# A fused attention and gated projection layer on one core: half steps filled by kind, and shift rows that go through DRAM

## The chip, the core and the metric

The kernel runs on one core of a Trainium2 chip, as one program. It uses the core's five engines: TensorE (PE) for matmuls, ScalarE (ACT) for activations, VectorE (DVE), GpSimd (POOL), and SyncE (SP), which here issues every DMA. The metric is the device time of one execution in microseconds; for the kernel before it is the median of three runs, 5673.93 us (5659.39 to 5677.47).

## What is computed

The input x has 8 batches of 2048 tokens with 512 channels in float32. The layer is, cut to what matters:

```
xn   = layernorm(x)                                  # over the 512 channels
q, k = xn Wq + bq, xn Wk + bk                        # 8 heads, 8 channels each
v    = xn Wv + bv                                    # 8 heads, 64 channels each
s    = leaky(q k^T / sqrt(8), slope 0.2)             # 2048 x 2048 per head
att  = gamma * softmax(s) v + xn
gate = softmax over 4 experts of a normalized projection of xn; only the largest is kept
g    = silu(xn W + sum over experts of gate * (xn Wd Wu))
out  = x + att * g
```

## The kernel before

**Tiling.** A block is 512 tokens, four to a batch (`NB`). Heads are taken in pairs, four to a batch (`NPAIR`). A *sequence* is one batch, one block of queries and one pair of heads: 16 a batch, 128 in all. A sequence runs over 16 *chunks* of 128 keys (`CH`). The main loop therefore has 2048 steps, one for each sequence s and chunk i.

**One step.** TensorE runs `less_max` for the first head of the pair (L658, adds the negated row maximum to the scores in PSUM), the scores of the next chunk (L641), the two matmuls of `max_unit` (L587, scores for a sequence further on, of which only the row maxima are kept by VectorE, L598), and `less_max` for the second head. ScalarE then takes exp of both heads (L670) and applies the leaky slope to the next scores (L652). The next step's `less_max` waits for that. Until then TensorE has time for other work: this is the *half step*. GpSimd adds each chunk's exponentials into the denominators (L702).

**What fills the half step.** First the *values* of earlier chunks: `weigh` multiplies exp scores by v (L682, one chunk is one matmul for each head) and may lag; chunks not yet weighed stand in the list `last`. Second, work from three queues of generators: `ending(s)` (denominators dps, L725; transposes of the result atp, L742; four VectorE operations, L744 to L749; output), `shift_rows` (below), and the background `behind()`, which runs through two kinds of blocks. `project_block` prepares the next batch: layer norm, transposes tp (L362, VectorE copy L365, ScalarE `normalize` L310), queries and keys (qkps, L257, split by VectorE at L323 and L326 and stored to DRAM), and values (vps, L271). `lift_block` computes g for one block of the current batch: pps (L257), norms nps (L422), dps (L257), gate gps (L443 and small VectorE operations), ranks rps (L490 and three VectorE operations L493, L496, L499), and four times zps (L271 and L510, then tanh th on ScalarE L513 and g on VectorE L514). All of these results pass through the one PSUM buffer of the pool `ps_m`, tag "m".

**Who decides.** A generator yields a state at each place where it may be interrupted: HOLD (in the middle of a chain of matmuls), WAIT (goes on at the next half step), FREE, SLOW, or IDLE (not yet). `background` steps through the queues until an estimated cost of 1.6 us is spent or the planner's due time (`due_at`, from a list of tasks with costs and ends) is met. The main loop then weighs zero, one or two chunks by what `background` spent. When loading of the next stacks (`load_stacks`, at i = 0 for sequence s + 2) finds that batch's keys not yet stored, it calls `background(force=True)` until they are. Layer norm statistics of the next block (`norm`: bn_stats L295 and L296) are advanced behind each vps and zps job through `following`.

**Shift rows.** For each sequence, `shift_rows` turns the row maxima (128 tokens on partitions) into rows along the free axis, split into a high and a low part. VectorE reduces (L604, L610, L611), GpSimd splits (L612 to L617), TensorE transposes the 128x16 result into PSUM (cps, L622), VectorE copies it to SBUF (cT, L624), and eight DMAs from SP lay it into the tile `shift` (L630). `less_max` of that sequence reads the tile.

**Order.** The order of instructions on each engine is the order in which the program issues them. A queue works strictly in order, so an instruction that waits holds everything behind it on its engine. SP likewise issues its DMAs in order.

Of the kernel before, what the change touches and what calls it, by code (L numbers as in the profile page):

```python
# [32 lines left out]
def fused_layer_kernel(  # L33
# [66 lines left out]

    xtiles = {}
# [54 lines left out]
    nc.gpsimd.memset(rx, 0.0)  # L156
    ones_r = const.tile([128, 128], FR, name="ones_r")
# [76 lines left out]

    EARLY = 9
    SLOW, WAIT, HOLD, FREE, IDLE = 4, 3, 2, 1, 0
# [46 lines left out]
    normed = {}  # L283
    ready = []
# [67 lines left out]
    def project_block(b, n, following, prefetch):  # L352

        if (b, n) not in normed:
            for _ in norm(b, n):
                pass
        xn, normalize = normed.pop((b, n))
        xnT = two.tile([128, NC, BLK], FP, name="xnT")
        for t in range(NT):
# [7 lines left out]
            yield FREE  # L367
# [20 lines left out]
        for t in range(NT):  # L388
            ps = bank([128, C], "vps")
            yield from token_major(ps, wv_sb, columns(xnT), t)  # L390
            add_bias(vb, t, ps)
            next(following, None)
            yield FREE
# [3 lines left out]
        if not prefetch:  # L397
            for _ in following:
                yield FREE
            yield FREE  # L400

    def lift_block(b, n, following, prefetch, cols=None):
# [16 lines left out]
        yield FREE  # L419
# [20 lines left out]
        yield FREE  # L440
# [45 lines left out]
        yield FREE  # L486
# [6 lines left out]
        nc.vector.tensor_tensor(rps, rps, dn, ALU.mult)  # L493
        dst = one.tile([128, BLK], FR, name="dst")
# [3 lines left out]
        )  # L498
        nc.vector.tensor_tensor(dst[64:128, :], rps[64:128, :], hi[64:128, :], ALU.subtract)  # L499
        spend(0.5)  # L500
        yield WAIT
        nc.scalar.copy(dst[0:64, :], hi[0:64, :])
        yield WAIT

        g = one.tile([128, NT, C], FP, name="g")
        for t in range(NT):
# [8 lines left out]
            next(following, None)  # L515
            yield SLOW
        nc.sync.dma_start(out=GS[b][n], in_=g)
        lifted.append((b, n))
        if not prefetch:
            for _ in following:  # L520
                yield FREE
            yield FREE
# [10 lines left out]
    def load_stacks(s):  # L533
# [4 lines left out]
        while b > 0 and b not in ready:  # L538
            background(force=True)
# [15 lines left out]
    def load_values(s):  # L555
# [3 lines left out]
        while b not in valued:  # L559
            background(force=True)  # L560
# [39 lines left out]
    def shift_rows(s):  # L600
# [7 lines left out]
        c = sm.tile([128, 2, 2 * NT], FP, name="c")  # L608
# [11 lines left out]
        yield FREE  # L620
        cps = ps_m.tile([4 * NT, 128], FP, name="cps", tag="m")
        nc.tensor.transpose(cps, c.rearrange("p i m -> p (i m)"), ident)  # L622
        cT = sm.tile([4 * NT, 128], FP, name="cT")
        nc.vector.tensor_copy(cT, cps)  # L624
        spend(0.45)
        shift = qp.tile([128, BLK], FR, name="shift")
        for g in range(4):
            for i in range(2):
                o = 2 * NT * i + NT * (g % 2)
                nc.sync.dma_start(  # L630
# [455 lines left out]
```

## Time and profile before

| what | value |
|---|---|
| median of three runs | 5673.93 us |
| profiled execution | 5658.03 us |
| its span, first to last instruction | 5656.3 us |
| TensorE busy | 5390.9 us, 95% |
| GpSimd busy | 4783.9 us, 85% |
| ScalarE busy | 4454.6 us, 79% |
| VectorE busy | 3643.2 us, 64% |
| DMA queue of SP | 35.4% of 16 engines, 109 GB/s |
| granted TensorE clock, mean | 0.978 |

In the profile, a row of instructions names the line of the kernel, the engine, the operation and the tiles (output <- inputs), then how often it ran, its busy time and the mean of one, and the idle time of the engine just before such instructions with what ended it. In the timeline, the first column is the start in microseconds from the span's start, the second the duration of the (merged) instructions; in brackets stands the idle time before and what released it. A float32 matmul shows two records for each instruction, so one chunk of values shows as four rows of L682, and two matmuls of a projection as four. A view by windows gives, for each stretch: its length, busy time of PE, PEld, DVE, ACT and POOL with the number of instructions in brackets, then the granted clock, the DMA share and GB/s.

### The profile page before, as it was taken

The page shows a single profiled execution, that of the slowest core. Times are in us where ns is not written, and L with a number is a line of the kernel's source. Part 1 is how long each engine was busy: PE and PEld are TensorE (multiplying, and loading weights), DVE is VectorE, ACT ScalarE, POOL GpSimd, SP SyncE. Part 2 cuts the span into 40 slices and gives each one's busy share as a digit, 9 for nine tenths or more (in the row PEclk, how much of TensorE's full clock was granted, in tenths as well). Part 3 has the DMA queues.
Part 4 walks back from the last instruction along what each step waited for, and adds up shares of the span by engine and source line. Part 5 has one row for each costly group of instructions (what it writes and reads, how often), then busy time and mean ns, then how long its engine had stood idle before and what let it go on. Part 6 is the DMA issues. An engine that isn't in the chain of part 4 may idle for free.

```text
span 5656.3 us, 78627 instructions
## 1 busy us (share of the span) xinstructions
PE 5390.9 (95%) x26386; PEld 1975.0 (35%) x26386; DVE 3643.2 (64%) x4988; ACT 4454.6 (79%) x8627; POOL 4783.9 (85%) x2904
## 2 busy tenths in 40 slices
PE   8899999999999999999999999999999999999998
PEld 3333333333333333333333333333333333333332
DVE  5566666667666665676666666667666666665664
ACT  2788878888788887888778887888878888777787
POOL 1789888888788987889788888888888898788888
PEclk9899999999999999999999999999999999999998
DMA  5324342343423333333333334233353243422221
GB/s 189 111 77 153 105 136 77 98 144 99 123 88 115 116 114 112 98 101 126 114 107 95 118 114 144 94 87 122 96 148 106 70 149 93 136 79 82 71 76 59
DMA packets 518026, 614.34 MB, mean 109 GB/s; under 512 B 30780, under 2 KB 429116, under 8 KB 481528
## 3 DMA queue, kind: packets, MB, share of 16 engines
q1 hardware_dynamic: 517624, 609.32, 35.4%
q8 instruction: 210, 3.44, 0.3%
q14 instruction: 192, 1.57, 0.1%
HBM read 405.79 MB, written 201.33 MB: 107 GB/s over the span
## 4 chain that ended last, share of the span: by engine, by line
PE 65%; DVE 16%; ACT 9%; issue 6%; POOL 2%; DMA 1%; SPq 0%; DVEq 0%; POOLq 0%; ACTq 0%
PE av L682 20%; PE sc L658 12%; PE vps L271 8%; PE zps L271 8%; PE mx L587 6%; DVE mxr L598 5%; ACT ex L670 5%; ACT sc L652 3%; PE qkps L257 3%; PE dps L257 2%; PE pps L257 2%; DVE gs L749 2%; DVE atp L748 2%; POOL acc L702 1%; DVE atp L744 1%
## 5 line engine op out<-in xcount | busy, mean ns | idle before, releaser
L702 POOL TENSOR_TENSOR acc<-acc,ex 128x1024 f32<-128x1024 f32 x1792 | 4236.9, 2364 | 294.8 <-ACT ex L670 201.8
L598 DVE TENSOR_REDUCE mxr<-mx 128x2 f32<-128x1024 f32 x2032 | 2481.7, 1221 | 1449.8 <-PE sc L658 1019.0
L670 ACT ACTIVATE ex<-sc 128x512 f32<-128x512 f32 x4096 | 2236.3, 597 | 962.3 <-PE sc L658 806.2
L652 ACT ACTIVATE sc<-sc 128x512 f32<-128x512 f32 x4096 | 2235.6, 592 | 20.1 <-PE sc L641 20.1
L682 PE MATMUL av<-ex,v_sb 128*64 128x512 f32 x8192 | 2122.0, 618 | 0.7
L658 PE MATMUL sc<-shift,ones_r 2*128 2x512 f32 x4096 | 1633.4, 458 | 74.3 <-ACT sc L652 70.3
L587 PE MATMUL mx<-k,q_sb 32*128 32x512 f32 x4096 | 1430.4, 449 | 27.7 <-DVE mxr L598 22.6
L658 PEld LDWEIGHTS sc<-shift,ones_r 2*128 2x128 f32 x4096 | 687.8, 185 | 1757.3 <-ACT sc L652 1696.0
L641 PE MATMUL sc<-q_sb,k 32*128 32x512 f32 x4096 | 1029.7, 499 | 0.0
L682 PEld LDWEIGHTS av<-ex,v_sb 128*64 128x64 f32 x8192 | 453.9, 136 | 775.0 <-issue 752.3
L587 PEld LDWEIGHTS mx<-k,q_sb 32*128 32x128 f32 x4096 | 563.7, 185 | 72.2 <-DVE mxr L598 57.1
L271 PE MATMUL zps<-w_sb,xnT 128*128 128x512 f32 (+1 forms) x1120 | 550.1, 606 | 16.9 <-DMA xnT<-XT 10.5
L702 POOL TENSOR_TENSOR acc<-ex 128x1024 f32<-128x1024 f32 x128 | 302.1, 2360 | 266.3 <-ACT ex L670 266.2
L271 PE MATMUL vps<-wv_sb,xnT 128*128 128x512 f32 x960 | 485.7, 627 | 12.2 <-DVE lo L326 10.8
L641 PEld LDWEIGHTS sc<-q_sb,k 32*128 32x128 f32 x4096 | 382.5, 183 | 0.8 <-issue 0.8
L271 PEld LDWEIGHTS zps<-w_sb,xnT 128*128 128x128 f32 x1120 | 190.4, 194 | 259.3 <-issue 192.4
L271 PEld LDWEIGHTS vps<-wv_sb,xnT 128*128 128x128 f32 x960 | 163.3, 190 | 217.2 <-issue 193.4
L514 DVE SCALAR_TENSOR_TENSOR g<-th,zps 128x512 f32<-128x512 f32 x128 | 88.0, 688 | 177.2 <-ACT th L513 177.2
L612 POOL TENSOR_TENSOR ml<-m,big 128x8 f32<-128x8 f32 x128 | 26.2, 205 | 144.3 <-DVE m L611 144.3
L257 PE MATMUL qkps<-xnT,wqk_sb 128*128 128x512 f32 x240 | 138.9, 716 | 7.6 <-DVE xnT L365 5.5
L257 PE MATMUL dps<-xnT,wd_sb 128*128 128x512 f32 (+1 forms) x280 | 135.0, 596 | 0.0
L257 PE MATMUL pps<-xnT,wp_sb 128*128 128x512 f32 (+1 forms) x280 | 133.4, 588 | 0.7
(125 smaller groups left out, 2648.4 us busy)
## 6 DMA issues: line engine op xcount, KB each, us to landing
v_sb<-VS SPq DMA_DIRECT2D x127, 1024.0 KB
k<-KS SPq DMA_DIRECT2D x256, 256.0 KB
XN<-xn SPq DMA_DIRECT2D x32, 1024.0 KB
q_sb<-QS SPq DMA_DIRECT2D x256, 128.0 KB
xnT<-XT SPq DMA_DIRECT2D x32, 1024.0 KB
GS<-g SPq DMA_DIRECT2D x32, 1024.0 KB
gs<-GS SPq DMA_DIRECT2D x128, 256.0 KB
xs<-in_x_dram SPq DMA_DIRECT2D x128, 256.0 KB
```

The costliest lines, as they stand in the source:

```text
L257: nc.tensor.matmul(ps[:, part], lhsT=wt[:, c, :], rhs=xnT[c][:, part], start=(c == 0 and part.start == 0), stop=(c == NC - 1 and part.stop ...
L271: nc.tensor.matmul(ps[:, part], lhsT=xnT[c][:, t * 128 : (t + 1) * 128], rhs=wt[:, c, part], start=(c == 0 and part.start == 0), stop=(c = ...
L587: nc.tensor.matmul(parts[e], lhsT=q_sb[r, t * 128 : (t + 1) * 128], rhs=k_sb[r, kb // 2 * BLK : (kb // 2 + 1) * BLK], start=True, stop=True,)
L598: nc.vector.reduce_max(mxr[s][:, :, t, kb : kb + 1], mx, axis=AX.X)
L641: nc.tensor.matmul(sc[e], lhsT=k_sb[r, i // 2 * 128 : (i // 2 + 1) * 128], rhs=q_sb[r, :], start=True, stop=True,)
L652: nc.scalar.activation(sc[e], sc[e], AF.Prelu, alpha=SLOPE)
L658: nc.tensor.matmul(sc[e], lhsT=ones_r[r, :], rhs=shifts[s][r, :], start=False, stop=True, skip_group_check=True,)
L670: nc.scalar.activation(ex[:, e, :], sc[e], AF.Exp, scale=qscale)
L682: nc.tensor.matmul(avt[s][64 * e : 64 * e + DV, :], lhsT=v_sb[:, i, 64 * e : 64 * e + DV], rhs=ex[:, e, :], start=(i == 0), stop=(i == CH ...
L702: nc.gpsimd.tensor_tensor(acc[s], old, ex, ALU.add)
L748: nc.vector.tensor_tensor(tp, tp, gs, ALU.mult)
L749: nc.vector.tensor_tensor(gs, tp, xs[:, 0], ALU.add)
```

## The change

The rule by which half steps are filled is replaced by two functions. In all but the last batch `half_full` decides by the kind of what is next: a WAIT piece goes on and one or two chunks are weighed; a small piece (new state TINY) comes behind one chunk of values; otherwise the half holds either two matmuls of a chain or two chunks of values. After a finished piece, values come first (`ended`). In the last batch `half_light` weighs about one chunk each step and fills up to 0.8 us of estimated cost. Layer norm statistics are kept in `stats` and advanced only in halves of values. `ranks` in `lift_block` is spread over two WAIT states more evenly: product, high part, low part. `load_stacks(s + 2)` may come at i = 0 to 3, and the queue is forced only at i = 3. The planner's allowance per sequence (`END`) goes from 1.45 to 1.0.

In `shift_rows` the TensorE transpose and the copy out of PSUM go away. VectorE transposes the tile `parts` in blocks of 32x32 (only 16 of its 32 columns are used), four DMAs write the result to a DRAM tile `SH`, and four DMAs read it back as rows.

The diff, cut to its core:

```diff
+    SH = [tc.dram_tile([2, 2, NT, 4, 32], FP, name=f"SH{i}") for i in range(2)]
...
-    SLOW, WAIT, HOLD, FREE, IDLE = 4, 3, 2, 1, 0
+    TINY, SLOW, WAIT, HOLD, FREE, IDLE = 5, 4, 3, 2, 1, 0
...
 (project_block)
-        if (b, n) not in normed:
-            for _ in norm(b, n):
-                pass
+        for _ in stats.pop((b, n)):
+            pass
...
-            yield FREE
+            yield TINY if t + 1 < NT else FREE
...
             add_bias(vb, t, ps)
-            next(following, None)
-            yield FREE
+            yield FREE if prefetch or t + 1 < NT else TINY
...
 (lift_block: before nps, before gps, before rps)
-        yield FREE
+        yield TINY
...
         nc.vector.tensor_tensor(rps, rps, dn, ALU.mult)
+        spend(0.5)
+        yield WAIT
...
+        yield WAIT
         nc.vector.tensor_tensor(dst[64:128, :], rps[64:128, :], hi[64:128, :], ALU.subtract)
-        spend(0.5)
-        yield WAIT
         nc.scalar.copy(dst[0:64, :], hi[0:64, :])
-        yield WAIT
+        yield HOLD
...
             nc.vector.scalar_tensor_tensor(g[:, t, :], th, 1.0, ps, ALU.add, ALU.mult)
-            next(following, None)
-            yield SLOW
+            yield SLOW if prefetch or t + 1 < NT else TINY
...
 (shift_rows)
-        c = sm.tile([128, 2, 2 * NT], FP, name="c")
+        c = parts[s % 2][:, 0 : 4 * NT].rearrange("p (i m) -> p i m", i=2)
...
-        yield FREE
-        cps = ps_m.tile([4 * NT, 128], FP, name="cps", tag="m")
-        nc.tensor.transpose(cps, c.rearrange("p i m -> p (i m)"), ident)
-        cT = sm.tile([4 * NT, 128], FP, name="cT")
-        nc.vector.tensor_copy(cT, cps)
-        spend(0.45)
+        cT = sm.tile([128, 32], FP, name="cT")
+        nc.vector.transpose(cT, parts[s % 2])
+        for q in range(4):
+            nc.sync.dma_start(
+                out=SH[s % 2][:, :, :, q, :].rearrange("i e t j -> (i e t) j"),
+                in_=cT[32 * q : 32 * q + 4 * NT, :],
+            )
         shift = qp.tile([128, BLK], FR, name="shift")
         for g in range(4):
-            for i in range(2):
-                o = 2 * NT * i + NT * (g % 2)
-                nc.sync.dma_start(
-                    out=shift[STK * g + i : STK * g + i + 1, :].bitcast(FP), in_=cT[o : o + NT, :]
-                )
+            nc.sync.dma_start(
+                out=shift[STK * g : STK * g + 2, :].bitcast(FP),
+                in_=SH[s % 2][:, g % 2].rearrange("i t q j -> i (t q j)"),
+            )
...
 (ending: the two states FREE become TINY)
...
+    def ahead():
+        return holder or [k for k in (1, 0, 2) if queue[k] is not None and state[k] != IDLE]
+
+    def go_on():
+        for j in range(3):
+            if queue[j] is not None and state[j] == IDLE:
+                go(j)
+        if holder and state[holder[0]] == WAIT:
+            go(holder[0])
+            return True
+        return False
+
+    def force():
+        j = ahead()[0] if ahead() else 2
+        go(j)
+
+    def values(count):
+        for w in last[:count]:
+            weigh(*w)
+        del last[:count]
+
+    def half_full():
+        run = 0
+        for w in last[:2]:
+            run += 1
+            if w[1] == CH - 1:
+                break
+        alone = run and last[0][1] == CH - 1
+        if go_on():
+            values(run)
+            return
+        j = (ahead() or [None])[0]
+        if j == 2 and state[2] != HOLD and spent[0] > due[0] + AHEAD:
+            j = None
+        if j is not None and state[j] == TINY:
+            values(min(run, 1))
+            go(j)
+            ended[0] = True
+        elif j is None or len(last) > MUCH - (state[j] != HOLD) or (ended[0] and run > 1):
+            ended[0] = False
+            for g in stats.values():
+                next(g, None)
+            values(run)
+        else:
+            if alone:
+                values(1)
+            go(j)
+            if state[j] == HOLD and not alone:
+                go(j)
+            ended[0] = state[j] != HOLD
+
+    def half_light():
+        begun = spent[0]
+        go_on()
+        late = last and (state[2] == SLOW or last[0][1] == CH - 1)
+        if late:
+            values(1)
+        j = (ahead() or [None])[0]
+        while j is not None and state[j] != WAIT and spent[0] < begun + 0.8 and (j < 2 or spent[0] < due[0]):
+            go(j)
+            if state[j] != HOLD:
+                break
+        if not late:
+            values(2 if spent[0] - begun < 0.4 and len(last) > 1 and last[0][1] < CH - 1 else 1)
+
+    MUCH, AHEAD = 3, 6.0
...
-    END = 1.45
+    END = 1.0
...
-                if i == 0:
+                if i <= 3 and s + 2 not in qst and (where(s + 2)[0] in (0, *ready) or i == 3):
                     load_stacks(s + 2)
...
+                if s < (B - 1) * SEQ:
+                    half_full()
                 else:
+                    half_light()
```

## The prediction

> **What bounds the kernel now.** I read the page first: shares by engine, then the groups.
>
> ```profile
> span 5656.3 us, 78627 instructions
> PE 5390.9 (95%) x26386; PEld 1975.0 (35%) x26386; DVE 3643.2 (64%) x4988; ACT 4454.6 (79%) x8627; POOL 4783.9 (85%) x2904
> L702 POOL TENSOR_TENSOR acc<-acc,ex 128x1024 f32<-128x1024 f32 x1792 | 4236.9, 2364 | 294.8 <-ACT ex L670 201.8
> L630 SPq DMA_DIRECT2D shift<-cT x1024: 572/573/1599, 127.8 to 5593.2; - x171
> ```
>
> TensorE looks full and GpSimd nearly so. But busy shares say little here, since matmuls overlap. So I cut the trace into the 2048 steps of the main loop: a step runs from one first `less_max` (L658) to the next, and its length is the distance between their starts. The first starts at 135.5 us, the last at 5639.6, and 16.6 us follow. The timeline shows three kinds. First two matmuls of a projection, then two chunks of values (TensorE alone):
>
> ```profile
> 569.03 0.49 PE L658 MATMUL sc<-shift,ones_r 2*128 2x512 f32 x1
> 569.69 1.99 PE L257 MATMUL pps<-xnT,wp_sb 128*128 128x512 f32 x4
> 571.61 0.49 PE L658 MATMUL sc<-shift,ones_r 2*128 2x512 f32 x1
> 572.27 1.94 PE L682 MATMUL av<-ex,v_sb 128*64 128x512 f32 x8
> 574.14 0.49 PE L658 MATMUL sc<-shift,ones_r 2*128 2x512 f32 x1
> ```
>
> 571.61 - 569.03 = 2.58 us, then 2.53: TensorE sets these. A step with one chunk alone:
>
> ```profile
> 941.30 0.49 PE L658 MATMUL sc<-shift,ones_r 2*128 2x512 f32 x1
> 941.89 1.09 ACT L670 ACTIVATE ex<-sc 128x512 f32<-128x512 f32 x2 [0.19 <-PE sc L658]
> 942.18 1.08 PE L682 MATMUL av<-ex,v_sb 128*64 128x512 f32 x4
> 942.86 1.09 ACT L652 ACTIVATE sc<-sc 128x512 f32<-128x512 f32 x2
> 943.52 0.50 PE L658 MATMUL sc<-shift,ones_r 2*128 2x512 f32 x1 [0.26 <-ACT sc L652]
> ```
>
> It takes 2.22 us, and its end is set by ScalarE (exp, then the leaky step of the next scores). So a step costs about 2.22 us however little TensorE has, and 2.55 with a full half. Last, a half step in which the queue is forced (start of a batch's last load of stacks), TensorE alone:
>
> ```profile
> 738.41 1.94 PE L682 MATMUL av<-ex,v_sb 128*64 128x512 f32 x8
> 740.93 0.66 PE L362 MATMUL tp<-ident,xn 128*128 128x128 f32 x4 [0.58 <-ACT xn L310]
> 742.46 0.63 PE L362 MATMUL tp<-ident,xn 128*128 128x128 f32 x4 [0.87 <-DVE xnT L365]
> ...
> 747.79 6.54 PE L257 MATMUL qkps<-xnT,wqk_sb 128*128 128x512 f32 x8 [0.78 <-DVE xnT L365]
> 754.26 0.50 PE L658 MATMUL sc<-shift,ones_r 2*128 2x512 f32 x1
> ```
>
> 754.26 - 737.51 = 16.75 us for one step; it occurs seven times.
>
> **The method.** I counted, in the order of instructions of both built programs, what each half step holds, and gave each kind the median length it has in this trace. The median is free of stalls; what actual lengths have over it is the stall. For the bulk, steps 16 to 1791 (sequences 1 to 111, up to the last batch):
>
> - two chunks, 2.53 us: 491 before, 613 after
> - two matmuls, 2.585: 431, 489; with L510 behind them, 2.81: 67, 93
> - a chunk and a matmul (some with L510), 2.73 to 2.96: 195, 30
> - a chunk and a small piece: 500, 418
> - a chunk alone, 2.22: 85, 103
> - one matmul (some with L510), 2.3 to 2.4 (estimate: the ScalarE floor and a little): 0, 30
> - forced: 7, 0
>
> **Part 1, the half steps by kind.** After, 613 x 2.53 + 489 x 2.585 + 93 x 2.81 + 30 x 2.73 + 103 x 2.22 + 30 x 2.36 = 3458 us. The 418 small ones: transposes of the input 84 x 2.66 + 28 x 2.36 (ScalarE's L310 is added there), denominators and final transposes 222 x 2.25, norms 28 x 2.7, gate 28 x 2.66, ranks 28 x 2.25 = 1002. Together 4460 us. Two of these kinds stand in the trace only the other way round (final transposes and ranks ahead of the chunk); their shortest cases, 2.24 and 2.26, are the price. The same sum for before is 4470: **the stall-free work is the same**, because the 128 removed L622 transposes lie in steps that ScalarE ends anyway. The actual bulk is 4782, so 312 us are stalls, and what the change is worth is how many go.
>
> - Forced halves: 7 x 16.45 - 7 x 2.53 = 97 us, and 18 in the steps behind them (L271 waits for L326). After, no half holds more than three matmuls: loading of stacks may wait until the fourth step of a sequence, and the program is never forced. Gone: 115.
> - Small piece ahead of the chunk: denominators 2.53 (91 of them), against 2.25 where the chunk is ahead (20): the small matmuls wait for VectorE or for the one PSUM bank "m", with the chunk behind them. All are turned round: 91 x 0.28 = 25 us; final transposes 2.51 against 2.25, 111 x 0.26 = 29; L622, 91 x 0.16 = 15. Gone: some 69.
> - Bank "m" and VectorE after a job's end: pairs of zps matmuls cost 52 us over price, 33 of it behind ranks (three 0.69 us VectorE operations in one go; the maxima's L598 comes late, and L587 waits for it). After, they are spread over three halves, every finished piece is followed by values, and bn_stats stand behind L598 instead of ahead. Of the 128 left (312 - 115 - 69) I take about 30 to remain.
> - New stalls: after denominators come final transposes at once, then four 0.69 us VectorE operations in two steps, in the steps where L604 to L611 also run: 2.96 + 2.8 us of VectorE against 2.25 + 2.53 of step, less about 0.6 of slack: 0.4 us x 111 = 45. Long runs of light steps, below: 25.
>
> Bulk after: 4460 + 30 + 45 + 25 = **4560**, 222 less. The last 255 steps are 666 us now. Priced with the medians of that stretch (half-size matmul and chunk 2.40), after comes to 610, and I leave 25 of stalls: 635, 31 less. Sequence 0 stays at about 55 us: its 15.4 us step waits for the load of xnT, which is untouched.
>
> [...]
>
> ```profile
> 737.00:757.00 20.00, 14.48 (x49) 6.37 (x46) 6.59 (x9) 8.14 (x15) 8.40 (x6) 0.74 0.43 152
> 1000.00:1040.00 40.00, 38.89 (x211) 14.80 (x207) 27.33 (x47) 33.13 (x66) 35.95 (x24) 1.00 0.36 106
> ```
>
> The column behind the brackets is the granted clock: 0.74 in a forced stretch, 1.00 in a normal one. In the trace's clock records it is halved 34 times; in light runs a lone chunk then takes 3.06 us for 2.22 and the first pair of matmuls up to 5.1 for 2.6. [...] If each of the 28 blocks fell, 28 x (3 x 0.84 + 2.5) = 140 us. But 13 runs of six light steps in the bulk now show no fall, and of 22 pairs of idlest steps one does. I take 25 us, five falls.
>
> **Part 2, the shift rows.** Removed per sequence: L622 (0.27 us), L624 (0.27), eight DMAs. Added: a 128x32 block transpose on VectorE (between L604's 0.19 and L624's 0.27; hidden, VectorE is at 64%), four DMAs to DRAM, a wait on SP for them, four back. At 0.62 us from issue to issue and 1.4 from an issue to its landing (L630 in the trace), the path is 4 x 0.62 + 1.4 + 4 x 0.62 + 1.4 = 7.8 us, 6.4 before. In the programs' order it now starts always in the tenth step; before, in the 11th to 14th. Six steps, 15 us, are left until the next sequence's first `less_max`. Queued behind SP's wait are stacks and values needed seven steps or more later. Cost nothing; without that cover, 127 x the lateness. Before the loop nothing covers it: +2 us.
>
> **GpSimd** does not take over: L702 queued starts every 2.44 us; 15 x 2.44 + 1.5 for L612 to L617 + 0.7 for norms = 38.8 us a sequence, against 4560 / 111 = 41.1.
>
> **Sum** against the profiled execution: 5656.3 - 222 - 31 + 2 = 5405 us of span. The execution took 5658.0, the median of the runs is 5673.9; keeping some of that distance, **5415 us**.
>
> **The rivals.**
> 1. The clock falls in most light runs (140 for 25): 5530. [...] Chance 0.15.
> 2. VectorE is late every sequence: denominators with final transposes right behind now cost 3.02 us for 2.25 (19 cases). If that stays, 111 x 0.77 = 85 for 45, and as much again in the maxima: 5455 to 5540, say 5500. The chunk between them (0.86 us) speaks against. Chance 0.08.
> 3. Slower: the round trip of the shift rows ends after the sequence. It has 7 us of slack; behind a burst of block stores (3 MB at 400 GB/s, 8 us, some two sequences a batch) it is used up. The gain of 251 is gone if all 127 sequences are 2 us late, at 17 us from transpose to landing; at 20 us, 5415 + 127 x 5 = 6050. Chance 0.07.
> 4. No change: forced work only moves, with its stalls (spread halves that wait for the same banks): 5670. Chance 0.03.
>
> The rest, 0.67, is the forecast, with 5340 to 5490 as its own range. The range over all but 2 in 10 is 5335 to 5550. About 0.3% is what a measurement can tell: faster 0.90, same 0.03, slower 0.07.
>
> **What would show it.** Right: no step over 6 us behind sequence 0; granted clock 0.99 in the bulk; no wait of L587 for L598 behind ranks; denominators and final transposes at 2.25. Wrong: L657, the new line of `less_max`, waiting for a DMA at each sequence's start; half clock in light runs; steps of pure pairs longer than 2.6.

## The result and the profile after

The changed kernel takes 5629.96 us (median of five runs, 5619.18 to 5640.99) against 5673.93 us: a ratio of 0.9927, 95% interval 0.9906 to 0.9948. It is faster, as forecast, but by 44 us where 259 were forecast, and it lies 80 us above the range.

First the page of the changed kernel: span, busy shares, the granted clock in 40 slices, and the group of the denominators' adds.

```profile
span 5617.4 us, 78032 instructions
PE 5378.9 (96%) x26258; PEld 1999.1 (36%) x26258; DVE 3673.9 (65%) x4988; ACT 4440.7 (79%) x8627; POOL 4779.1 (85%) x2906
PEclk9999999999999999999999999999999999979989
L701 POOL TENSOR_TENSOR acc<-acc,ex 128x1024 f32<-128x1024 f32 x1792 | 4231.0, 2361 | 301.7 <-ACT ex L669 189.3
```

The busy shares have hardly moved. TensorE's busy time fell by 12 us only, although 128 transposes (35 us) are gone: more of its work ran at half clock (mean granted clock 0.968, before 0.978). The same cut into steps as in the prediction (from one first `less_max`, now L657, to the next), in us:

| stretch | before | predicted | after |
|---|---|---|---|
| to the first step | 135.5 | 137.5 | 131.2 |
| sequence 0 | 55.9 | 55 | 59.9 |
| bulk, steps 16 to 1791 | 4781.8 | 4560 | 4702.8 |
| last 255 steps | 666.4 | 635 | 704.8 |
| tail | 16.6 | 17 | 18.8 |
| span | 5656.3 | 5405 | 5617.4 |

So the missing 212 us lie in two places: 143 in the bulk and 70 in the last batch. With the prediction's prices the bulk's steps come to 4461 us, so that 241 us of stalls are left, where 100 were allowed. (That the sum agrees with the 4460 forecast tests little, since counts and prices are the forecast's own. With the medians of the changed kernel's trace the same steps come to 4517: some 57 of the 241 us are steps that are dearer in the median.) The seven forced half steps of 16.45 us are gone. But steps over 6 us are not. In six sequences of the bulk one step takes 7.4 to 8.9 us. Here is one of them in the timeline of the changed kernel (start, duration):

```profile
2062.25 1.48 SPq L717 DMA_DIRECT2D xs<-XN  x1
...
2065.55 0.70 DVE L743 TENSOR_TENSOR atp<-atp,rd 128x512 f32<-128x512 f32 x1
...
2067.99 0.49 PE L657 MATMUL sc<-shift,ones_r 2*128 2x512 f32 x1
...
2069.69 0.70 DVE L744 TENSOR_TENSOR atp<-atp,xs 128x512 f32<-128x512 f32 x1 [3.43 <-DMA xs<-XN]
2070.29 1.22 DVE L597 TENSOR_REDUCE mxr<-mx 128x2 f32<-128x1024 f32 x1
2071.57 0.80 PE L586 MATMUL mx<-k,q_sb 32*128 32x512 f32 x2 [3.08 <-DVE mxr L597]
...
2072.71 3.68 PE L681 MATMUL av<-ex,v_sb 128*64 128x512 f32 x8
...
2076.32 0.79 PE L657 MATMUL sc<-shift,ones_r 2*128 2x512 f32 x1
```

The step is 2076.32 - 2067.99 = 8.33 us. An ending reads `gs` and `xs` back from DRAM (L714 to L717). Between 2053 and 2059 us SP has just issued the stores of a whole block (KS, QS, XN, XT), and this read, issued at 2062.25, is waited for until 2069.69. Behind the 3.43 us of this wait VectorE does L744 and then the row maxima (L597, at 2070.29), which need nothing of the read. TensorE's next maxima (L586) wait 3.08 us for those, and then two chunks take 3.68 us for 1.94, at a granted clock of 0.50. In the view of waits (us in total, times, longest) of the kernel before, where VectorE waits for no such read, and then of the changed kernel:

```profile
PE mx L587 <- DVE mxr L598: 22.6, 69, 0.7
```

```profile
PE mx L586 <- DVE mxr L597: 35.9, 20, 3.7
...
DVE atp L744 <- DMA xs<-XN: 25.9, 8, 4.0
```

In the last batch it is another wait. The timeline of the changed kernel around one gate and ranks:

```profile
5016.13 0.69 DVE L748 TENSOR_TENSOR gs<-atp,xs 128x512 f32<-128x512 f32 x1
...
5016.97 1.84 PE L446 MATMUL gps<-simn,pw 128*128 128x4 f32 x8 [3.02 <-DVE gs L748]
...
5018.74 1.98 PE L681 MATMUL av<-ex,v_sb 128*64 128x512 f32 x4
...
5020.64 0.79 PE L657 MATMUL sc<-shift,ones_r 2*128 2x512 f32 x1
...
5027.38 1.12 PE L493 MATMUL rps<-ident,rx 128*128 128x128 f32 x4 [2.45 <-DVE rx L479]
```

`half_light` lets the ending's last two VectorE operations and the gate's first matmuls fall into one half. Both need the one PSUM bank "m". TensorE waits 3.02 us with the chunk behind the gate, then runs at a granted clock of 0.50: one chunk takes 1.98 us for 1.08. The steps with norms, gate and ranks take 6.0 to 7.6 us each here, 2.3 to 4.2 before.

The shift rows, on the other hand, are in time. Timeline of the changed kernel, one round trip:

```profile
5023.04 0.20 DVE L621 STREAM_TRANSPOSE cT<-c 128x32 f32<-128x32 f32 x1
...
5023.27 1.70 SPq L623 DMA_DIRECT2D SH<-cT  x4
...
5026.09 1.11 SPq L629 DMA_DIRECT2D shift<-SH  x4
```

The last read is issued 4.2 us after the start of the transpose. No `less_max` waits for a DMA anywhere in the view of waits.

### The profile page after: what moved, and what is told of

It is laid out like the page before. It is cut to its first block, busy times and chain, and to the rows that moved or that the text cites. A ratio compares the mean times of both kernels' runs of the same rounds, so it can differ in the third digit from the quotient of the medians.

```text
span 5617.4 us, 78032 instructions
## 1 busy us (share of the span) xinstructions
PE 5378.9 (96%) x26258; PEld 1999.1 (36%) x26258; DVE 3673.9 (65%) x4988; ACT 4440.7 (79%) x8627; POOL 4779.1 (85%) x2906
## 4 chain that ended last, share of the span: by engine, by line
PE 80%; ACT 8%; DVE 7%; DMA 2%; issue 2%; SPq 1%; POOL 1%; POOLq 0%; ACTq 0%; DVEq 0%
PE av L681 28%; PE sc L657 16%; PE zps L279 9%; PE vps L279 8%; PE mx L586 7%; ACT ex L669 5%; ACT sc L651 2%; PE pps L265 2%; DVE mxr L597 2%; PE qkps L265 2%; PE dps L265 2%; PE dps L724 1%; DMA xs<-XN 1%; PE atp L741 1%; DVE gs L748 1%
## 5 line engine op out<-in xcount | busy, mean ns | idle before, releaser
L597 DVE TENSOR_REDUCE mxr<-mx 128x2 f32<-128x1024 f32 x2032 | 2480.2, 1221 | 1260.0 <-PE sc L657 1018.5
L681 PE MATMUL av<-ex,v_sb 128*64 128x512 f32 x8192 | 2149.5, 630 | 11.6 <-DVE avs L708 9.2
L657 PE MATMUL sc<-shift,ones_r 2*128 2x512 f32 x4096 | 1679.7, 463 | 75.5 <-ACT sc L651 66.9
L586 PE MATMUL mx<-k,q_sb 32*128 32x512 f32 x4096 | 1445.4, 454 | 37.0 <-DVE mxr L597 35.9
L657 PEld LDWEIGHTS sc<-shift,ones_r 2*128 2x128 f32 x4096 | 703.6, 187 | 1560.4 <-ACT sc L651 1450.5
L681 PEld LDWEIGHTS av<-ex,v_sb 128*64 128x64 f32 x8192 | 469.7, 138 | 839.6 <-issue 805.2
L586 PEld LDWEIGHTS mx<-k,q_sb 32*128 32x128 f32 x4096 | 562.2, 188 | 61.2 <-DVE mxr L597 49.4
L349 DVE TENSOR_TENSOR vb<-vps,bv_sb 128x512 f32<-128x512 f32 x120 | 83.0, 691 | 95.6 <-PE vps L279 95.4
```

The lines of the kernel that those rows point to most:

```text
L349: nc.vector.tensor_tensor(vb[:, :, t, :], ps.rearrange("p (h d) -> p h d", h=NPAIR), bv_sb.rearrange("p (h d) -> p h d", h=NPAIR), ALU.add,)
L586: nc.tensor.matmul(parts[e], lhsT=q_sb[r, t * 128 : (t + 1) * 128], rhs=k_sb[r, kb // 2 * BLK : (kb // 2 + 1) * BLK], start=True, stop=True,)
L597: nc.vector.reduce_max(mxr[s][:, :, t, kb : kb + 1], mx, axis=AX.X)
L657: nc.tensor.matmul(sc[e], lhsT=ones_r[r, :], rhs=shifts[s][r, :], start=False, stop=True, skip_group_check=True,)
L681: nc.tensor.matmul(avt[s][64 * e : 64 * e + DV, :], lhsT=v_sb[:, i, 64 * e : 64 * e + DV], rhs=ex[:, e, :], start=(i == 0), stop=(i == CH ...
```

## Experiments

All versions compute the whole layer. "Half-clock steps" are steps touched by a stretch in which the trace's clock records show half the clock; before has 32 in the bulk and 30 in the last batch, after 64 and 46. Ratios are to the kernel before, with 95% intervals. Lines of the edits are in the changed kernel unless said otherwise.

A trace is one execution, and two traces differ. The version with earlier reads and the one with reads and pause, both below, give TensorE the same work in the same order up to the last batch; yet their traces show 4655.6 and 4680.2 us of bulk, and 41 and 62 half-clock steps in it. So a difference of some 25 us or 20 such steps between two traces shows nothing by itself. Whether a version is faster is read from the ratios.

### The two parts alone

Edit 1: the kernel before with the new `shift_rows` (tile `parts`, `SH`, eight DMAs through DRAM), and the planner's allowance that goes with it.

```diff
-        cps = ps_m.tile([4 * NT, 128], FP, name="cps", tag="m")
-        nc.tensor.transpose(cps, c.rearrange("p i m -> p (i m)"), ident)
...
+        nc.vector.transpose(cT, parts[s % 2])
...
-    END = 1.45
+    END = 1.0
```

> The kernel before, with only the shift rows taken through DRAM (VectorE transpose, four writes, four reads, END 1.0). Theory A (the half-step rule is what moves the time, the shift rows only free TensorE of a small piece): within 20 us of the kernel before, 5655 to 5695, because the removed transposes lie in steps that ScalarE or VectorE ends, and the seven forced halves stay. Theory B (the round trip through DRAM keeps SP waiting and is what ate the forecast gain): slower than before by 40 us or more, with waits of the first less_max of a sequence on a DMA.

Measured: 5782.99 us, ratio 1.0195 (1.0149 to 1.0241): slower by 2%. The time is theory B's, but not for B's reason: `less_max` waits for a DMA three times only, 1.5 us in all. The forced half steps are still there, though shorter (10.3 us in the median), and endings wait for a DMA. From the view of waits of this run (its L752 is L744 above):

```profile
DVE atp L752 <- DMA xs<-XN: 70.0, 7, 10.9
```

Seven times VectorE waits some 10 us for an ending's reads, issued behind a block's stores and the loads of the next stacks, and half-clock steps in the bulk go from 32 to 103.

Edit 2: the changed kernel with the old shift rows as a TINY piece, `END = 1.45`, and a list in which an ending waits while the one before it is unfinished (without it the program runs out of half steps).

```diff
-        nc.vector.transpose(cT, parts[s % 2])
...
+        yield TINY
+        cps = ps_m.tile([4 * NT, 128], FP, name="cps", tag="m")
...
-    END = 1.0
+    END = 1.45
```

> The changed kernel with the old shift rows (TensorE transpose as a small piece behind one chunk, copy, eight DMAs, END 1.45); an ending that comes while one is still running waits in a list. Theory A: the extra 111 small halves take the room that the rule needs, seven forced stretches come back, and the time is 5660 to 5700, no better than before; so the two parts of the change need each other. Theory B (round trip costs): 5560 to 5600, faster than the changed kernel.

Measured: 5906.33 us, 1.0393 (1.0344 to 1.0441), slower than either theory had it. Forced stretches are back (five of 18.2 to 19.5 us, one of 22.1), as theory A said. In seven steps behind them, of 13.8 to 14.7 us, TensorE waits 9.2 to 9.8 us for the stacks whose load came so late (`q_sb<-QS`). The edit changes three things at once, so it shows only that the new rule had no room for 111 more small pieces here, not the worth of one part.

### The late reads

Edit: in `ending`, five half steps instead of three between the issue of the reads and the denominators.

```diff
-        for _ in range(3):
+        for _ in range(5):
             yield IDLE
```

> The changed kernel with five idle halves instead of three between the reads of an ending (gs, xs) and its denominators. Theory A (in eight to twenty sequences the reads stand behind a block's stores, VectorE waits for them in order, TensorE for VectorE, and its clock halves): the A2 steps of 5 to 9 us behind the final transposes are gone, bulk shorter by 40 to 60 us, 5570 to 5595 us in all. Rival (VectorE is late from its own work, not from the reads): the A2 steps stay at 2.7 us on the mean, gain under 10 us.

Measured: 5577.10 us, 0.9828 (0.979 to 0.9867). VectorE no longer waits for any DMA in the main loop. The bulk is 4655.6 us, 47 less (23 less in the trace of the version with the pause, below), and half-clock steps in it go from 64 to 41 (to 62 there). The ratio is 1.0% lower, as theory A had it.

The same edit on the shift rows alone, with the waiting list:

> The kernel before with the shift rows through DRAM, as in the first experiment, and five idle halves instead of three between the reads of an ending and its use (an ending that comes while one runs waits in a list). Theory A (what made that kernel 110 us slower are seven waits of 10 us of VectorE for the ending's reads, which come earlier in the sequence once no TensorE piece of the shift rows stands ahead, and the falls of the clock behind them): 70 to 110 us less than 5783, 5670 to 5715. Rival (the round trip itself holds SP and the sequence's start): 5770 or more.

Measured: 5673.60 us, 1.0008 (0.9986 to 1.0031). So the slow result of the first experiment came from the late reads, as theory A had it. With reads in time, this version takes as long as the kernel before. That is a balance, not proof that no part of it matters: the forced half steps take 6.3 us here for 16.45, seven times, and against that stand 77 half-clock steps in the bulk for 32.

### The last batch

Edit: when `half_light` has just gone on with a waiting piece, it weighs one chunk and begins nothing new.

```diff
         begun = spent[0]
-        go_on()
+        if go_on():
+            values(1)
+            return
```

> The changed kernel; in the last batch a half step in which a waiting piece went on takes one chunk of values and nothing new. Theory A (norms, gate and ranks of the last batch are sent to TensorE while VectorE still has the PSUM bank, and the clock halves behind that): the last 255 steps go from 705 to about 640 us, 5565 us in all. Rival (the last batch is long because its halves are too light for the clock whatever the order): 690 or more, 5615 in all.

Measured: 5585.36 us, 0.9846 (0.9801 to 0.9891). The last 255 steps go from 704.8 to 659.4 us (theory A had 640). The window view (length, busy PE, PEld, DVE, ACT, POOL, then granted clock) of the changed kernel over the last batch:

```profile
4920.00:5580.00 660.00, 609.74 (x2906) 224.62 (x2904) 366.82 (x476) 500.87 (x975) 540.18 (x311) 0.89 0.24 72
```

and of this run, which gets more done in the same 660 us (2994 matmul records for 2906):

```profile
4920.00:5580.00 660.00, 621.79 (x2994) 228.55 (x2990) 371.22 (x485) 519.59 (x1011) 569.54 (x324) 0.91 0.25 75
```

Both edits together:

> The changed kernel with five idle halves ahead of an ending's denominators and with the pause in the last batch. If the late reads and the last batch are separate causes, their gains (45 and 45 us of span) add: 5528 us of span, 5535 as a median. If they share a cause, 5560 to 5575.

Measured: 5535.03 us, 0.9764 (0.9745 to 0.9784): the two gains add (1.0% and 0.8% of the kernel alone, 1.6% together). This version is the base of the next five runs.

### The clock in light steps

First a matmul of 256 columns ahead of the row maxima in each step behind a light half, alone and on the base:

```diff
...
+        if warm:
+            nc.tensor.matmul(parts[0][:, 0:256], lhsT=ones, rhs=bv_sb[:, 0:256], start=True, stop=True)
```

> The changed kernel with one more 128x128 by 256 column matmul of constants ahead of the maxima in each step that follows a half with one chunk alone, or with norms or gate (its result is overwritten by the maxima). Theory A (in runs of light steps TensorE's clock falls to half because it is too idle, and a light step then takes 3.06 us for 2.22): the half-clock light steps go, 5617 to about 5560 us, granted clock in the bulk from 0.98 to 0.99; the falls behind late reads stay. Rival (the light steps are long for another reason, VectorE): 0.43 us more in some 230 steps, no step gets shorter, 5620 to 5700.

> All three: five idle halves, the pause in the last batch, the warm matmul. Theory A: what is left over the stall-free price in light steps goes too, about 40 us below the kernel without the warm matmul: 5490 us, near the forecast's range. Rival: no better than without it, 5530 or more.

Measured: 5813.56 us, 1.0253 (1.0225 to 1.0280), and 5642.30 us, 0.9963 (0.9942 to 0.9983). On the base, half-clock steps fall from 62 to 47 and from 29 to 17, but the matmul lies between `less_max` and exp. It makes its step 0.7 us longer where a chunk is alone (2.96 for 2.22) and 1.05 where a pair is (3.59 for 2.54). Right about the clock and wrong about the place. So a smaller one was put where TensorE idles, behind the lone chunk (0.23 us in the run of light steps below); it adds zeros to 128 columns of the sum of values:

```diff
...
+                light = weighed - len(last) == 1 and spent[0] - before in (0.0, 1.0)
+                if light and newest[1] < CH - 1:
+                    nc.tensor.matmul(
+                        avt[newest[0]][0:64, 0:128], lhsT=zeros, rhs=bv_sb[:, 0:128], start=False, stop=False
+                    )
```

> The version with early reads and the pause in the last batch, and in light steps (a chunk alone, or with norms or the gate) behind the chunk one small matmul that adds zeros to 128 columns of the running sum of values; TensorE has about 0.26 us free there. Theory A (the clock halves because TensorE idles too much in runs of light steps): the bulk's steps under half clock fall from about 60 to under 30, light steps alone return from 2.48 mean to 2.3, and the time goes from 5535 to 5480 to 5500. Rival B (idle time of this size is not what decides, the clock falls behind longer waits elsewhere): as many steps under half clock, and 5535 to 5560, since some 290 small matmuls of about 0.2 us cost nothing to half of that.

Measured: 5497.61 us, 0.9677 (0.9649 to 0.9705), about 0.9% below the base. Half-clock steps fall from 62 (41 in the other trace of this bulk) to 28 and from 29 to 13; steps with a chunk alone from 2.36 (2.33) to 2.23 us on average, since none of them is touched any more. The bulk is 31 us (7) shorter although the matmul costs 0.37 us each behind norms and gate (49 of them, 18 us). A run of light steps on the base, timeline and window:

```profile
2223.09 0.49 PE L657 MATMUL sc<-shift,ones_r 2*128 2x512 f32 x1 [0.95 <-ACT sc L651]
...
2224.01 1.08 PE L681 MATMUL av<-ex,v_sb 128*64 128x512 f32 x4
2225.31 0.72 PE L657 MATMUL sc<-shift,ones_r 2*128 2x512 f32 x1 [0.23 <-ACT sc L651]
...
2226.54 1.98 PE L681 MATMUL av<-ex,v_sb 128*64 128x512 f32 x4
2228.44 1.08 PE L724 MATMUL dps<-acc,ones 128*32 128x256 f32 x8
2229.45 0.79 PE L657 MATMUL sc<-shift,ones_r 2*128 2x512 f32 x1
```

```profile
2225.00:2252.00 27.00, 26.77 (x92) 8.59 (x92) 15.69 (x28) 15.76 (x31) 20.02 (x15) 0.51 0.14 38
```

and the same place with the small matmul (its L1064; `less_max` is L659 here):

```profile
2222.87 0.38 PE L1064 MATMUL av<-bv_sb,zeros 128*64 128x128 f32 x2
2223.27 0.50 PE L659 MATMUL sc<-shift,ones_r 2*128 2x512 f32 x1
...
2224.19 1.08 PE L683 MATMUL av<-ex,v_sb 128*64 128x512 f32 x4
2225.20 0.64 PE L726 MATMUL dps<-acc,ones 128*32 128x256 f32 x8
2225.76 0.50 PE L659 MATMUL sc<-shift,ones_r 2*128 2x512 f32 x1
```

```profile
2223.00:2250.00 27.00, 26.82 (x141) 10.53 (x139) 21.01 (x34) 23.24 (x46) 24.82 (x17) 1.00 0.30 83
```

On the base the clock falls at about 2225.4 with no idle time of TensorE longer than 0.95 us ahead of it, stays at 0.51 for 27 us, and the chunk with denominators takes 4.14 us. With 0.38 us of zeros in the gaps it stays at 1.00, and that step takes 2.5 us. TensorE looks just as busy in both windows (26.77 and 26.82 of 27 us), but does 92 records in one and 141 in the other.

**What the falls go with.** The clock records of all sixteen traces change on a grid of 3.41 us. For each window of that grid, from the second sequence on, I estimated its *fill* from the shapes in the records. Each matmul record counts with 0.43 us for 512 columns of float32, the distance between the records of one projection in these traces, and with half of that where a matmul has a single record (`less_max`, scores, maxima, L510). This is weighted with rows/128 x output columns/128 of its shape (128*128 is the largest in the traces) and given as a share of the window at full clock. The limits in the table are those at which these traces part.

| clock in the window | fill (estimate) | windows | clock changes behind it |
|---|---|---|---|
| full | below 0.30 | 181 | 180 |
| full | 0.30 to 0.42 | 894 | 291 |
| full | above 0.42 | 23062 | 0 |
| half | below 0.35 | 426 | 6 |
| half | 0.35 to 0.45 | 641 | 321 |
| half | above 0.45 | 138 | 138 |

TensorE's busy share sorts them worse: 33 of the 471 falls come behind windows that are over 95% busy. On the base, the window ahead of the fall is filled 0.33 and 65% busy; the first seven at half clock are filled 0.34 to 0.37, the eighth 0.40, and behind that the clock rises. So in these traces the clock goes with the estimated fill more closely than with how long TensorE is busy; why it does, no trace shows. A window of light steps that catches only one chunk gets 0.25 from it by the estimate, and what its other matmuls add decides in which row it falls. The zeros of one step add only 0.03, and the step two ahead of the fall is also shorter there (2.33 us for 2.69); which of the two keeps the clock up in such places isn't shown.

### The order within a half step

Edit on the base: the small piece ahead of its chunk again, as the kernel before mostly had it.

```diff
         if j is not None and state[j] == TINY:
-            values(min(run, 1))
             go(j)
+            values(min(run, 1))
```

> The version with early reads and the pause, with one thing undone: a small piece (denominators, final transposes, norms, gate, ranks) is again put ahead of its chunk of values. Theory A (the prediction's step: each costs 0.26 to 0.28 us more that way, 111 denominators and 111 final transposes, input transposes nothing): 5535 + 60 = 5595, denominators with a chunk at 2.53. Rival B (the order within the half is worth nothing, since the second less_max of the step and ScalarE set it): 5525 to 5550, denominators with a chunk at 2.25 to 2.35.

Measured: 5510.94 us, 0.9699 (0.9669 to 0.9728): some 0.7% *faster* than the base, which neither theory gave; its price for the denominators is theory A's. An ending in this run:

```profile
1179.91 0.49 PE L657 MATMUL sc<-shift,ones_r 2*128 2x512 f32 x1
...
1180.86 0.64 PE L724 MATMUL dps<-acc,ones 128*32 128x256 f32 x8 [0.20 <-POOL c L614]
1181.43 1.08 PE L681 MATMUL av<-ex,v_sb 128*64 128x512 f32 x4
1182.44 0.49 PE L657 MATMUL sc<-shift,ones_r 2*128 2x512 f32 x1
...
1183.10 0.66 PE L741 MATMUL atp<-ident,avs 128*128 128x128 f32 x4
1183.68 1.08 PE L681 MATMUL av<-ex,v_sb 128*64 128x512 f32 x4
1184.69 0.50 PE L657 MATMUL sc<-shift,ones_r 2*128 2x512 f32 x1
```

Denominators with a chunk take 1182.44 - 1179.91 = 2.53 us (median 2.52; 2.25 on the base), as priced in the prediction. Final transposes take 2.25 us here (median 2.27; 2.47 on the base), the opposite of the price. Half-clock steps in the bulk fall from 62 (41) to 25, and windows filled less than 0.35 from 14 (8) to 3; none of the 101 steps with a chunk alone is touched (mean 2.22, 2.36 on the base). The same work, in another order, leaves fewer windows with little in them.

Edit on the base: one half step of values between denominators and final transposes.

```diff
         spend(0.5)
+        yield WAIT
         yield TINY
         tp = ps_m.tile([128, NT, 128], FP, name="atp", tag="m")
```

> The version with early reads and the pause, and in every ending one half step of values between denominators and final transposes (two light steps no longer follow each other). Theory A (the 2.47 us of final transposes, against the 2.25 that the prediction took, come from the light step right ahead, in which ScalarE's work is drawn together and VectorE still works on the denominators): final transposes with a chunk at 2.25 to 2.30, less 111 x 0.2 = 22 us: 5513. Rival B (the final transposes cost 2.45 wherever they stand, for VectorE's operations of that step): no change there, 5530 to 5545.

Measured: 5595.69 us, 0.9849 (0.9825 to 0.9874), slower. The price is as theory A had it: final transposes fall from 2.47 to 2.26 in the median. But there are more light steps (a chunk alone 119 times for 101), half-clock steps in the bulk rise from 62 to 80, and input transposes go from 2.60 to 3.15 us on average.

Small pieces ahead and zeros (behind lone chunks only) together:

> Early reads, the pause in the last batch, small pieces ahead of their chunk, and the small zero-adding matmul behind steps with a chunk alone (not behind norms and gate, where it made a step 0.37 us longer). Theory A (both keep the clock up, in different places: the order in the bulk, the zeros in the last batch and behind gate and ranks): 5465 to 5490, steps under half clock under 15 in the bulk and under 20 in the last batch. Rival B (they mend the same falls, the second adds nothing): 5500 to 5520, about 25 and 40 such steps, as with the order alone.

Measured: 5492.79 us, 0.969 (0.9664 to 0.9717). Half-clock steps are 16 and 12, but the bulk (4639.8 us) is hardly below the order alone (4645.1), and the total is that of the zeros alone: in the bulk the two seem to mend the same falls, though differences this small lie within those between two traces. The last 255 steps take 633 us.

### VectorE held by GpSimd

Still open was why pairs of chunks stayed at 2.63 to 2.71 us on average for 2.53. The timeline of the base behind one ending:

```profile
1003.74 2.17 DVE L609 TENSOR_SCALAR big<-m 128x8 f32<-128x8 f32 x1
...
1006.02 0.69 DVE L743 TENSOR_TENSOR atp<-atp,rd 128x512 f32<-128x512 f32 x1
1006.74 0.70 DVE L744 TENSOR_TENSOR atp<-atp,xs 128x512 f32<-128x512 f32 x1
1007.35 1.22 DVE L597 TENSOR_REDUCE mxr<-mx 128x2 f32<-128x1024 f32 x1
```

with GpSimd at that time

```profile
1001.06 4.81 POOL L701 TENSOR_TENSOR acc<-acc,ex 128x1024 f32<-128x1024 f32 x2
```

and TensorE

```profile
1006.40 0.49 PE L657 MATMUL sc<-shift,ones_r 2*128 2x512 f32 x1
1008.62 0.50 PE L586 MATMUL mx<-k,q_sb 32*128 32x512 f32 x2 [1.73 <-DVE mxr L597]
...
1009.29 2.75 PE L681 MATMUL av<-ex,v_sb 128*64 128x512 f32 x8
```

L609 works on 128x8 numbers. It takes 0.16 us as a rule and 2.17 here: it ends with the GpSimd add (1001.06 + 4.81 = 1005.87, L609 at 1005.91). The hold does not appear as a wait, only as a long duration. In the bulk of the changed kernel 19 of 111 sequences have it: L609 starts 0.54 to 1.84 us ahead of the end of an add, takes 0.57 to 1.87 us and ends 0.03 us after the add. In the bulk before, none of 111 has: 28 start under an add, all in its last 0.26 us, and the longest takes 0.29. In the four steps from it on, the time over price is 3.03 us, in the other 92 sequences 1.07. The group of this operation before, and after:

```profile
L610 DVE TENSOR_SCALAR big<-m 128x8 f32<-128x8 f32 x128 | 24.4, 190 | 0.1
```

```profile
L609 DVE TENSOR_SCALAR big<-m 128x8 f32<-128x8 f32 x128 | 51.3, 401 | 0.0
```

What holds the operation, the trace does not show; it shows the two ends 0.03 us apart. If it is the running add, VectorE is not held where the operation is GpSimd's. Edit: the two small operations on GpSimd, on the changed kernel, and on the last version above (both mends of light steps).

```diff
-        nc.vector.tensor_scalar(big, m[:, :, 0], 0.0, SLOPE, ALU.min, ALU.mult)
-        nc.vector.tensor_scalar_max(m[:, :, 0], m[:, :, 0], 0.0)
+        nc.gpsimd.tensor_scalar(big, m[:, :, 0], 0.0, SLOPE, ALU.min, ALU.mult)
+        nc.gpsimd.tensor_scalar_max(m[:, :, 0], m[:, :, 0], 0.0)
```

> The changed kernel with one edit: the leaky slope on the row maxima (two operations on 128x8 numbers in each sequence) runs on GpSimd in place of VectorE. Theory A (VectorE held behind a running GpSimd add makes the maxima late, and the clock falls behind some of these): in the profile of the changed kernel the 19 sequences of the bulk with a held operation are 3.03 us over price in the four steps behind, the 92 others 1.07, so 19 x 2 = 37 us less, somewhat fewer where late reads hold VectorE anyway: 5595 to 5610 against 5630. Rival B (VectorE has slack there, the reads alone make it late): 5620 to 5635.

> The version with early reads, pause, small pieces ahead and the zero-adding matmul, and the leaky slope on the row maxima on GpSimd in place of VectorE. Theory A: 21 sequences with a held operation are 1.46 us over price in four steps against 0.64, so 17 us less, 5475 against 5493. Rival B: within 6 us of it, since the two operations that GpSimd gets instead (0.2 us each and their waits) shift its adds.

Measured: 5582.41 us, 0.9828 (0.9796 to 0.9861) on the changed kernel, and **5453.31 us, 0.9604 (0.9571 to 0.9637)** on the best version, which beats both kernels. Each gains about 0.9 to 1.0%. On the changed kernel the bulk is 34 us shorter, which is theory A's 37; the ratio's 1.0% is more, but its interval covers 37 us. On the best version the bulk falls from 4639.8 to 4610.0 us, and half-clock steps from 16 and 12 to 11 and 11; the 0.9% is clear of theory A's 17 us, and why was not settled. The edit also takes two operations (0.33 us in each sequence) off VectorE, held or not; the share of that was not measured apart.

## Why the prediction was right or wrong

**Right: the direction and the forced half steps.** The seven forced steps went. The prices held for most kinds of step; with the medians of the changed kernel the sum of 4460 us is 4517, and 24 of these 57 us are the final transposes (below).

**Right: the shift rows are in time.** No `less_max` of the changed kernel waits for a DMA, and the version with this part alone and reads in time is at 1.0008 (0.9986 to 1.0031), though as a balance of gains and losses. The terms of the path were too dear: four writes took 1.70 us and four reads 1.11 on SP, for 4 x 0.62 = 2.48 each. Before the loop it gave 4 us and did not cost 2. The third rival falls with it.

**Wrong: "new stalls: 45 + 25" and "about 30 to remain".** The 100 us that these allow were 241. Four things were missing or mis-sized:
- Late reads were in no term. The step "queued behind SP's wait are stacks and values needed seven steps or more later" looked at what stands behind the shift rows, but not at the endings' own reads behind a block's stores. Their mend took 23 to 47 us off the bulk, by the two traces, and 1.0% off the kernel.
- VectorE's stalls were priced as too much work in two steps (2.96 + 2.8 us). The trace shows a hold instead: in 19 of 111 sequences L609 starts 0.54 to 1.84 us ahead of the end of a GpSimd add, where before it started in the gaps between the adds or in their last 0.26 us. With the operation on GpSimd, 34 us of the bulk (4702.8 to 4668.8) and 1.0% of the whole kernel went. The second rival saw VectorE late behind the denominators, and its price came in small: final transposes right behind them are 0.22 us dearer, where it had 0.77.
- The clock (25 us). The evidence was 13 light runs without a fall, mostly with the small piece ahead of the chunk. No run shows this term by itself; by the clock records half clock cost the bulk at most 60 us before, in 20 stretches, and 80 after, in 25. The change turned that order round, and the version with the order turned back has 25 half-clock steps where the base has 62 and 41 in its two traces. Evidence from one order was carried to another. The first rival had the right cause and the wrong size: the granted clock of 0.983 over 4702.8 us bounds the cost of half clock in the bulk at 80 us, against its 140, which took a fall around gate and ranks in each of the 28 blocks. And TensorE's busy share was not the measure (33 of 471 falls come behind windows over 95% busy): the estimated fill of a window sorts the falls better.
- Final transposes with a chunk ahead were priced at 2.25, from their shortest cases. They cost 2.47 where the denominators are in the step right before: 111 x 0.22 = 24 us. With a half step between, they cost 2.26. The kernel before had 19 cases of that order (final transposes right behind a chunk and denominators), at 3.02 us on average; the prediction knew them, but only as a rival.

**Wrong: "small piece ahead of the chunk … gone: some 69".** The price of the denominators held (2.52 against 2.25). But turning all pieces round again made the kernel 0.7% faster: 30 us lost at the denominators and 22 won at the final transposes by their medians; the rest goes with fewer falls of the clock. This term of the sum, 69 us of gain, had the wrong sign on this base.

**Wrong: "priced with the medians of that stretch … 610, and I leave 25 of stalls".** The last 255 steps took 705 us for 635. The wait for the bank "m" in `half_light` and the half clock behind it make up most of the difference: with the pause it is 659, with reads and pause 647, with light steps mended 633.

**The signs named in advance.** "No step over 6 us" failed, and so did a granted clock of 0.99 in the bulk (0.983; 0.988 before). "No wait of L587 for L598 behind ranks" held as to ranks but not behind endings; denominators at 2.25 held, final transposes did not. Of the signs against, half clock in light runs came true; pure pairs stayed at 2.54 to 2.58 in the median and were 2.66 to 2.71 on average; no `less_max` waited for a DMA.

**The balance.** In ratios to before, times 5674 us: changed kernel 5633, reads and pause 5540, light steps mended 5498, L609 moved 5449, prediction 5415. Of the 215 us missed, the mends recover some 180. Not all of that need be what the change cost: whether the same mends would help the kernel before was tried for the reads with the shift rows alone, where they took back a loss and gave no gain, and not for the others. About 35 us stay unexplained.

## What to carry to other kernels

A median price per kind of step carries the work of a new schedule over, but not its stalls: for each operation that moves, ask what now runs beside it, what stands ahead of it in its queue and who has its bank, and look for a small operation whose *duration*, not wait, has grown (L609, 0.16 to 1.87 us in the changed kernel). Give reads that must be back by a fixed step a lead over the stores ahead of them: here one was waited for until 7.4 us after its issue, and two half steps more ended VectorE's waits for DMAs in the main loop. Evidence on the clock did not carry over to another order of the same work (62 and 41 half-clock steps in the bulk, 25 with the small pieces ahead); in these traces the estimated fill of each 3.41 us sorted the falls better than TensorE's busy share. Where light steps remain, a small matmul behind the lone chunk paid for itself here (0.9%), and one on the path to the next engine did not (2.0% slower than the base). And compare two traces of the same work before reading a small difference between two kernels.

## What was not expected of the hardware

- Half clock lasts in whole units of 3.41 us: 40 of the 41 stretches in the changed kernel, up to 27.3 us. On the base the clock fell with no idle time over 0.95 us ahead of it, and a stretch went on through 27 us in which the profile has TensorE 99% busy. By the estimate above, a fall comes behind 180 of the 181 windows filled below 0.30, behind 291 of the 894 from 0.30 to 0.42, and behind none of the 23062 above.
- A VectorE operation of 0.16 us (L609) took up to 1.87 us in the bulk of the changed kernel, and 2.17 behind one ending of the base, under a GpSimd add, and ended 0.03 to 0.04 us after it.
- A read of 256 KB on SP's queue was waited for until 7.4 us after its issue behind a block's stores, and with the shift rows alone VectorE waited for one up to 10.9 us.
